# When VectorE's transposition and a pair of statistics take their turn: an edit of the spectrum phase in a convolution and recurrence kernel

## The chip, the cores and the metric

The kernel runs on one core of one Trainium2 chip. A core has five engines that work at the same time, each through its own queue of instructions in order: TensorE (PE in the profile, with PEld for its weight loads), VectorE (DVE), ScalarE (ACT), GpSimd (POOL) and SyncE (SP). Transfers between memory and the core's SBUF are issued from the queues of SP, ACT and POOL; an engine that must wait for another waits on a semaphore, and everything behind the waiting instruction in its queue waits too. The metric is the device time of one execution in microseconds (us); lower is better.

## The reference

The input x is 4 images of 64 channels and 256 by 256 pixels, all in float32. Two layers are added to it in turn. The edit lies in the first. Cut to what matters:

```python
def layer0(x):                                     # x + layer0(groupnorm(x))
    hidden = einsum('bchw,oc->bohw', x, w1)        # 1x1 convolution, 64 -> 384 channels
    hidden = depthwise_3x3(hidden, w_dw)
    q, k, v = split(hidden, 3, axis=1)             # 128 channels each
    out = irfft2(rfft2(patches_8x8(q)) * rfft2(patches_8x8(k)))   # circular convolution of each patch
    out = layernorm_over_channels(out) * ln_w + ln_b
    return einsum('bchw,oc->bohw', v * out, w_out) # 128 -> 64 channels
```

The second layer normalizes the result again in groups of channels and runs a recurrent cell (GRU) over the columns of the image; each column's state feeds the next. The group norm of an image needs the mean and variance of the whole image before the image's first pixel can be normalized.

## The kernel before, in words

The first layer takes about 3,600 us of the span and the second the rest. The first layer's loop is over 32 blocks (`for n in range(NBLK + 1)`, L617), 8 to an image; a block is 32 rows of the image, cut into 128 patches of 8 by 8 pixels with a halo of one pixel. The 3x3 convolution and the Fourier transform of a patch are one matrix product: for each channel a 100 by 64 matrix takes the patch with its halo to the 64 numbers of its spectrum. These matrices are streamed from memory (`fetch`, tile t).

A block goes through these phases, all in one program order:

1. First 1x1 phase (L632): 16 units, each a group of TensorE products into PSUM and one copy to the tile h, by ScalarE or, in two units, VectorE.
2. First spectrum phase (L657, `circular(n, 0, beside_first)`): four quarters, sp = 0 to 3. In each, TensorE transforms 16 channels of q and of k; ScalarE copies q's spectrum to a slot of the tile wk; VectorE makes two products of q and k (`products`, L400). After sp = 1 and after sp = 3 GpSimd adds the cross terms of two quarters (`crossed`, L410). After sp = 2 TensorE transforms the first two quarters back (`inverse`, L431).
3. Second 1x1 phase (L663): 16 units for the next channels. Unit 7 and unit 12 are copied by VectorE. After unit 11 the previous block's output is projected with w_out (`project`, L551) and VectorE adds the residual (`add_residual`, L568, four instructions); after unit 13 the rows leave for memory (`leave`, L579). Behind unit 15 comes the second inverse (`flush`).
4. Second spectrum phase (L679), third 1x1 phase (L683), and the phase of the values (L704).

PSUM is one ring of 8 banks (`psum`, L220). A transform or a unit takes two banks, an inverse or a projection four. TensorE can write a place again when whoever reads it is done. Followed through a block: the transform of k in quarter 3 takes the banks of k in quarter 2 and so waits for VectorE's two products of quarter 2. Units 14 and 15 of the second 1x1 phase take the four banks of the projection and wait for `add_residual`. The second inverse takes the banks of units 12 and 13 and waits for their copies.

Beside this main work VectorE does the layer norm of the *previous* block in small steps, one for each call of `go()` (L612). The generator `layer_norm` (L472) yields after each step; the last eight steps are transpositions, in turn of z and of v, for channel groups 0 to 3 (`turned`, L515). Seen from the first spectrum phase, z and v of groups 0 and 1 are done, and the four that are left are z2, v2, z3, v3. When group i is turned, `gated(n - 1, i)` (L527) scales z on ScalarE and multiplies it into v on GpSimd; the projection needs all four.

The third strand is the statistics of the *next* image, in blocks 0 to 23. GpSimd's queue fetches a piece of that image, 128 partitions by 1024 numbers, into one slot of wk called `seen` (`look`, L596). VectorE takes statistics of it with two instructions, and in the same call the next piece is fetched into the same slot:

```python
        def count(n, w):
            for i in range(2):
                nc.vector.bn_stats(bn0[:, w // 2 + i, :], seen[:, 512 * i : 512 * i + 512])
            if w == 12:
                nc.vector.bn_aggr(st0[:, n % 8, :], bn0)
            else:
                look(n, w + 4)
```

There are four pieces in a block: `look(n, 0)` stands at the block's start, and `count` at w = 0, 4, 8 and 12 in the first spectrum phase (sp = 1), the second 1x1 phase (unit 9), the second spectrum phase (sp = 2) and the third 1x1 phase (unit 2).

A class around the engines (`InOrder`, L146) keeps each engine's instructions in the order in which the program states them. Its method at L158 records every instruction, so the profile shows L158 for all of them; they are told apart by engine, operation and tiles (psring is the ring in PSUM; `bn<-wk` a statistic of `seen` or of rows that leave; `v<-v,z` the gate's product; `wk<-wk` a cross sum; `wk<-in_x` on POOL a `look`).

Of the kernel before, what the change touches and what calls it, by code (L numbers as in the profile page):

```python
# [163 lines left out]
def tile_conv_then_gru(  # L164
# [48 lines left out]
    with layer0 as s:  # L213
# [36 lines left out]
        def keep_matrices(queue, i, k0, k1):  # L250
            queue.dma_start(
                t_all[i, :, k0:k1].rearrange("p n k -> p (n k)"),
                ts[i][:, 16 * k0 : 16 * k1].rearrange("p c k -> p (c k)"),
            )
# [115 lines left out]
        def pointwise(n, chunk, unit, vector):  # L370

            unit_of(n, chunk, unit, vector)()
# [37 lines left out]
        def crossed(pair):  # L410

            slot = PAIRS[pair % 2][1]
            both = wk[:, slot : slot + 2]
            nc.gpsimd.tensor_tensor(both[:, :, 0:512], both[:, :, 0:512], both[:, :, 512:1024], ALU.add)
# [12 lines left out]
        def flush():  # L427
            while pending:
                pending.pop(0)()
# [97 lines left out]
        def gated(n, i):  # L527
            f = slice(32 * i, 32 * i + 32)
            nc.scalar.activation(
                z[:, :, f],  # L530
                z[:, :, f],
                AF.Identity,
                bias=ln_sb[:, 1, i : i + 1],
                scale=ln_sb[:, 0, i : i + 1],
            )
            nc.gpsimd.tensor_tensor(v[:, :, f], v[:, :, f], z[:, :, f], ALU.mult)
# [3 lines left out]
        def residual(n, u):  # L540
            b, r0 = n // 8, (n % 8) * 32 + u * 8
            xr = [wk[:, i].rearrange("p (r c) -> p r c", c=P) for i in (6, 2)]
            for g in range(2):
                for s in range(2):
                    nc.sync.dma_start(
                        xr[g][s * C : (s + 1) * C],
                        x[b, :, r0 + 16 * g : r0 + 16 * g + 8, s * P : s * P + P],
                    )
            return xr

        def project(n, u):  # L551
            po = psum(4)
            y = v.rearrange("p n (b k) -> p b n k", k=32)
            for b in range(4):
                for r in range(4):
                    for s in range(2):
                        n0 = 32 * u + 16 * s
                        nc.tensor.matmul(
                            po[s * 64 : s * 64 + 64, r].rearrange("p (n k) -> p n k", k=32),
                            lhsT=wo_sb[32 * r : 32 * r + 32, b, :],  # L560
                            rhs=y[32 * r : 32 * r + 32, b, n0 : n0 + 16],
                            start=b == 0,
                            stop=b == 3,
                            tile_position=(32 * r, s * 64),
                        )
            return po

        def add_residual(u, po, xr):  # L568
            for g in range(2):
                grid = xr[g].rearrange("p (h r) (n c) -> p h n r c", h=2, c=8)  # L570
                for half in range(2):
                    nc.vector.tensor_tensor(
                        grid[:, half],
                        po[:, 2 * g + half].rearrange("p (n r c) -> p n r c", r=4, c=8),
                        grid[:, half],
                        ALU.add,
                    )
# [18 lines left out]
        def look(n, w):  # L596

            nc.gpsimd.dma_start(seen, piece(x, n // 8 + 1, n % 8, w, 4))
# [8 lines that stand above are left out]
# [5 lines left out]
        def go(steps=1):  # L612
            for _ in range(steps):
                if norm:
                    next(norm, None)

        for n in range(NBLK + 1):  # L617
            last = n == NBLK
            more = not last and n // 8 + 1 < B
            if last:  # L620
                for _ in norm:
                    pass
                for i in range(4):
                    gated(n - 1, i)
                for u in range(2):
                    xr = residual(n - 1, u)
                    add_residual(u, project(n - 1, u), xr)
                    leave(n - 1, u, xr)
                break
            if more:  # L630
                look(n, 0)
            for unit in range(16):  # L632
                if unit < 14:
                    pointwise(n, 0, unit, unit in (3, 9) if norm else unit % 2)
                elif unit == 14:
                    last_two = [unit_of(n, 0, unit, False)]
                else:
                    last_two.append(unit_of(n, 0, unit, False))
                    for span in ((0, 16), (16, P)):
                        for copy in last_two:  # L640
                            copy(*span)
                if unit in (0, 3, 6, 9, 12):
                    go()
                if n == 0 and unit == 15:
                    keep_matrices(nc.gpsimd, 2, 0, 8)

            def beside_first(sp):
                if n and sp < 3:
                    gated(n - 1, sp)
                go()  # L650
                if n and sp == 3:
                    gated(n - 1, sp)
                if more and sp == 1:
                    count(n, 0)

            go()
            circular(n, 0, beside_first)  # L657
            crossed(1)
            go(8)
            xr = [None, None]  # L660
            if n:
                xr[0] = residual(n - 1, 0)
            for unit in range(16):  # L663
                pointwise(n, 1, unit, unit in (7, 12))
                if n and unit == 11:
                    add_residual(0, project(n - 1, 0), xr[0])
                if n and unit == 13:
                    leave(n - 1, 0, xr[0])
                if more and unit == 9:
                    count(n, 4)  # L670
            flush()
            norm = layer_norm(n)

            def beside(sp):
                go()
                if more and sp == 2:
                    count(n, 8)

            circular(n, 1, beside)  # L679
            image = None  # L680
            if n:
                xr[1] = residual(n - 1, 1)
            for unit in range(16):  # L683
                pointwise(n, 2, unit, unit in (4, 6, 15))
                if more and unit == 2:
                    count(n, 12)
                    if n % 8 == 7:
                        t = wk[:, 3]
                        nc.gpsimd.dma_start(t[:, 0 : 2 * P].rearrange("p (a q) -> p a q", a=2), sums)
                        image = norm_of_pieces(nc, st0, t, lambda: psum()[:, :, 0], eps, sc0[:, n // 8 + 1])  # L690
                if image and unit in (4, 8, 12):
                    next(image)
                if unit == 3:
                    flush()
                if unit in (6, 7):
                    go()
                if unit % 4 == 3 and n + 1 < NBLK:
                    load(n + 1, unit // 4)
            po = project(n - 1, 1) if n else None
            go(1)  # L700
            if n:
                add_residual(1, po, xr[1])
            go(3)
            for k in range(8):  # L704
                if k in (0, 3, 6):
                    pv = psum(4)
                    values(n, k, pv[:, 0:2])
                elif k in (1, 4, 7):
                    values(n, k, pv[:, 2:4])
                    keep_values(k - 1, 2, pv)  # L710
                else:
                    pv = psum()
                    values(n, k, pv)
                    keep_values(k, 1, pv)
                if k in (1, 2, 4) and n + 1 < NBLK:
                    normalize(n + 1, k // 2)
                if k == 5 and n:
                    leave(n - 1, 1, xr[1])
                if k == 5 and n + 1 < NBLK:
                    normalize(n + 1, 3)  # L720
                if k in (6, 7):
                    go()
            fetch(n * 24 + 28)
# [251 lines left out]
```

## Time and profile before

| | |
|---|---|
| median of 3 runs | 5094.03 us (5087.31 to 5103.36) |
| the profiled execution: its time, its span | 5097.92 us, 5096.1 us |
| granted TensorE clock, mean | 0.993 |
| PE matmuls busy | 4858.1 us, 95% |
| PEld weight loads busy | 4237.7 us, 83% |
| DVE busy | 4035.9 us, 79% |
| ACT busy | 3317.3 us, 65% |
| POOL busy | 1727.2 us, 34% |

The span is from the first to the last instruction of the profiled execution. Busy times of engines overlap. In a line of the timeline stand the start in us, the duration in us, the engine, the operation with the tile written, the arrow and the tiles read, shapes, the number of like instructions merged into the line, and in brackets how long the engine was idle just before and which engine's work ended that idle time.

### The profile page before, as it was taken

The numbers are of one execution on the slowest core, as the hardware profiler recorded it, in microseconds if no ns is written. First come the engines' busy times: TensorE is split into PE (matmuls) and PEld (weight loads), VectorE is DVE, ScalarE is ACT, GpSimd is POOL, SyncE is SP. The second block draws the span as 40 slices with busy tenths as digits, with TensorE's granted clock in tenths as the row PEclk, the third lists the DMA queues.
The fourth block names the chain that finished last, engine by engine and source line by source line (L and its number), as shares of the span: only waits on it lengthen the run. The fifth ranks groups of instructions, "written<-read, shape, count | busy, mean of one in ns | idle before, by whom it ended". The sixth has DMA issues, their size and how long they took to land.

```text
span 5096.1 us, 276113 instructions
## 1 busy us (share of the span) xinstructions
PE 4858.1 (95%) x127092; PEld 4237.7 (83%) x127092; DVE 4035.9 (79%) x7001; ACT 3317.3 (65%) x4269; POOL 1727.2 (34%) x1717
## 2 busy tenths in 40 slices
PE   6999999999999999999999999999879999999999
PEld 4888888888888888888888888888669999999998
DVE  5788888877888888788888877778867777777777
ACT  4666666666666666666666666666556666666665
POOL 0233333333333334333333333323343333333333
PEclk9999999999999999999999999999989999999999
DMA  8577676676777667677676666666443333333332
GB/s 306 162 189 191 186 191 182 180 183 187 187 195 196 170 184 187 179 190 191 186 195 168 173 161 174 173 171 180 121 125 103 104 103 103 102 104 103 103 103 73
DMA packets 435056, 823.57 MB, mean 162 GB/s; under 512 B 37156, under 2 KB 300068, under 8 KB 431364
## 3 DMA queue, kind: packets, MB, share of 16 engines
q1 hardware_dynamic: 380600, 582.13, 43.3%
q0 software_dynamic: 52432, 223.12, 14.7%
q8 instruction: 997, 16.33, 1.4%
q14 instruction: 163, 1.34, 0.1%
q10 hardware_dynamic: 864, 0.66, 0.0%
HBM read 660.53 MB, written 145.23 MB: 158 GB/s over the span
## 4 chain that ended last, share of the span: by engine, by line
PE 87%; ACT 4%; issue 4%; DVE 3%; DMA 2%; POOL 1%; SPq 0%; POOLq 0%; ACTq 0%; DVEq 0%
PE psring L158 62%; PE pshr L158 9%; PE pshz L158 8%; PE psni L158 6%; PE pshn L158 2%; ACT v L158 1%; ACT z L158 1%; DVE wk L158 1%; ACT xq L158 1%; DMA t<-t_all 1%; DVE z L158 1%; DMA t_all<-wk 0%; DVE lnst L158 0%; ACT h L158 0%; POOL v L158 0%
## 5 line engine op out<-in xcount | busy, mean ns | idle before, releaser
L158 PEld LDWEIGHTS psring<-h,t 100*32 100x32 f32 x49152 | 1385.9, 119 | 251.6 <-issue 214.5
L158 PE MATMUL psring<-h,t 100*32 100x128 f32 x49152 | 1463.5, 257 | 104.2 <-issue 69.4
L158 PEld LDWEIGHTS psring<-w_sb,xq 64*100 64x100 f32 x24576 | 1358.6, 163 | 107.9 <-issue 76.5
L158 PE MATMUL psring<-w_sb,xq 64*100 64x128 f32 x24576 | 1412.4, 271 | 23.0 <-issue 8.7
L158 ACT COPY h<-psring 100x1024 f32<-100x1024 f32 (+2 forms) x1371 | 1231.5, 990 | 308.0 <-PE psring L158 307.4
L158 DVE TENSOR_TENSOR wk<-psring,wk 128x1024 f32<-128x1024 f32 (+1 forms) x768 | 759.5, 1037 | 480.1 <-PE psring L158 346.4
L158 POOL TENSOR_TENSOR v<-v,z 128x2048 f32<-128x2048 f32 x128 | 582.9, 4558 | 664.5 <-DVE wk L158 603.5
L158 DVE TENSOR_TENSOR z<-z,moments 128x2048 f32<-128x2048 f32 x256 | 578.0, 2278 | 2.3
L158 POOL TENSOR_TENSOR wk<-wk 128x1024 f32<-128x1024 f32 x128 | 303.5, 2371 | 622.3 <-DVE wk L158 607.9
L158 POOL TENSOR_TENSOR raw<-raw,st 128x512 f32<-128x512 f32 x256 | 303.2, 1184 | 540.1 <-DVE st L158 424.6
L158 ACT COPY z<-psring 128x2048 f32<-128x2048 f32 (+1 forms) x144 | 248.4, 1725 | 343.9 <-PE psring L158 262.6
L158 ACT ACTIVATE z<-pshz,b_rz 128x288 f32<-128x288 f32 (+7 forms) x510 | 242.1, 475 | 339.2 <-PE pshz L158 334.1
L158 ACT COPY wk<-psring 128x1024 f32<-128x1024 f32 (+1 forms) x272 | 268.9, 988 | 288.5 <-PE psring L158 237.1
L158 PE MATMUL pshr<-st,wi 64*64 64x144 f32 (+7 forms) x12240 | 448.8, 270 | 6.9 <-DVE st L158 6.5
L158 PE MATMUL pshz<-st,wi 64*64 64x144 f32 (+7 forms) x12240 | 444.2, 269 | 0.9 <-issue 0.9
L158 PE MATMUL psni<-st,wi 64*64 64x144 f32 (+7 forms) x12240 | 444.0, 269 | 0.1
L158 DVE COPY h<-psring 100x1024 f32<-100x1024 f32 (+1 forms) x230 | 278.1, 1210 | 191.9 <-PE psring L158 188.1
L158 PEld LDWEIGHTS pshr<-st,wi 64*64 64x64 f32 x12240 | 378.0, 133 | 49.7 <-DVE st L158 36.9
L158 ACT COPY v<-psring 128x2048 f32<-128x2048 f32 (+2 forms) x176 | 251.9, 1436 | 254.3 <-PE psring L158 254.3
L158 DVE BATCH_NORM_STATS2 lnst<-z 128x6 f32<-128x128 f32 x2048 | 416.8, 281 | 0.0
L158 PEld LDWEIGHTS psni<-st,wi 64*64 64x64 f32 x12240 | 389.4, 133 | 21.9 <-issue 0.2
L158 PE MATMUL psring<-wk,g_sb 32*64 32x512 f32 x6144 | 386.7, 599 | 15.1 <-issue 12.1
(91 smaller groups left out, 6258.4 us busy)
## 6 DMA issues: line engine op xcount, KB each, us to landing
t<-t_all SPq DMA_DIRECT2D x768, 448.0 KB, 4.6
xq<-in_xh POOLq DMA_DIRECT2D x124, 800.0 KB, 5.2
wk<-in_x SPq DMA_DIRECT2D x256, 256.0 KB, 8.1
x<-wk POOLq DMA_DIRECT2D x256, 256.0 KB, 5.0
wk<-in_x POOLq DMA_DIRECT2D x96, 512.0 KB, 6.9
raw<-x SPq DMA_DIRECT2D x128, 256.0 KB, 3.0
raw<-x SPq DMA_DIRECT2D x256, 128.0 KB, 3.1
out<-raw SPq DMA_DIRECT2D x128, 256.0 KB, 2.7
```

The costliest lines, as they stand in the source:

```text
L158: return self.tc.keep_in_program_order(got(*args, **kwargs))
```

## The change

Two edits. In the first spectrum phase the four calls of `go()` become 0, 2, 1 and 1 steps: quarter 0 has none, and quarter 1 has two, so that the transposition of z2 stands behind the products of quarter 1, directly ahead of that of v2. And `count(n, 0)`, with its two statistics and the fetch of the next piece that it issues, moves from behind quarter 1 to behind unit 1 of the second 1x1 phase; `count(n, 4)` stays at unit 9. The first edit holds for blocks 1 to 31, the second for blocks 0 to 23. The computation is the same.

```diff
             def beside_first(sp):
                 if n and sp < 3:
                     gated(n - 1, sp)
-                go()
+                go((0, 2, 1, 1)[sp])
                 if n and sp == 3:
                     gated(n - 1, sp)
-                if more and sp == 1:
-                    count(n, 0)
...
                 if n and unit == 13:
                     leave(n - 1, 0, xr[0])
-                if more and unit == 9:
-                    count(n, 4)
+                if more and unit in (1, 9):
+                    count(n, unit // 9 * 4)
```

## The prediction

> **What bounds the kernel now.** I read the page's chain of work that ended last first, then the timeline of one block, engine by engine. Block 9, from 1107 us on, serves as the example.
>
> ```profile
> PE 87%; ACT 4%; issue 4%; DVE 3%; DMA 2%; POOL 1%; SPq 0%; POOLq 0%; ACTq 0%; DVEq 0%
> ```
>
> TensorE holds 87% of the chain. An edit on VectorE or GpSimd moves the time only where TensorE waits for it, so I look for those places in TensorE's own timeline:
>
> ```profile
> 1107.71 10.86 PE L158 MATMUL psring<-h,t 100*32 100x128 f32 x384 [0.36 <-ACT h L158]
> 1118.51 1.97 PE L158 MATMUL psring<-wk,g_sb 32*64 32x512 f32 x32
> 1120.94 1.16 PE L158 MATMUL psring<-wk,g_sb 32*64 32x512 f32 x16 [0.46 <-POOL wk L158]
> 1122.03 3.98 PE L158 MATMUL psring<-h,t 100*32 100x128 f32 x128
> 1125.94 10.83 PE L158 MATMUL psring<-w_sb,xq 64*100 64x128 f32 x192
> 1136.71 3.69 PE L158 MATMUL psring<-v,wo_sb 32*64 32x512 f32 x64
> 1140.33 3.79 PE L158 MATMUL psring<-w_sb,xq 64*100 64x128 f32 x64
> 1144.13 2.83 PE L158 MATMUL psring<-wk,g_sb 32*64 32x512 f32 x48
> ```
>
> These are the first spectrum phase (six transforms, the inverse in two parts, two transforms), units 0 to 11 of the second 1x1 phase, the projection, units 12 to 15 and the second inverse. The only waits in 40 us are 0.46 us for GpSimd's cross sum, and the last two transforms, 3.98 us where other blocks show 3.70. VectorE over the same stretch:
>
> ```profile
> 1111.55 2.36 DVE L158 TENSOR_TENSOR wk<-psring,wk 128x1024 f32<-128x1024 f32 x2 [1.28 <-PE psring L158]
> 1113.83 2.30 DVE L158 STREAM_TRANSPOSE z<-z 128x2048 f32<-128x2048 f32 x1
> 1116.05 2.32 DVE L158 TENSOR_TENSOR wk<-psring,wk 128x1024 f32<-128x1024 f32 x2
> 1118.29 2.29 DVE L158 STREAM_TRANSPOSE v<-v 128x2048 f32<-128x2048 f32 x1
> 1120.51 1.24 DVE L158 BATCH_NORM_STATS2 bn<-wk 128x6 f32<-128x512 f32 x2
> 1121.67 2.34 DVE L158 TENSOR_TENSOR wk<-psring,wk 128x1024 f32<-128x1024 f32 x2
> ...
> 1134.43 1.28 DVE L158 BATCH_NORM_STATS2 bn<-wk 128x6 f32<-128x512 f32 x2
> 1140.46 2.48 DVE L158 TENSOR_TENSOR wk<-psring,wk 128x512 f32<-128x512 f32 x4 [4.75 <-issue]
> ```
>
> The last two lines are today's second count (unit 9) and the four residual adds, which start 0.07 us after the projection's end at 1140.39. GpSimd, behind its cross sum for quarters 0 and 1:
>
> ```profile
> 1125.35 0.60 POOL L158 DMA_DIRECT2D wk<-in_x  x1
> 1125.97 4.55 POOL L158 TENSOR_TENSOR v<-v,z 128x2048 f32<-128x2048 f32 x1
> 1130.89 4.51 POOL L158 TENSOR_TENSOR v<-v,z 128x2048 f32<-128x2048 f32 x1 [0.37 <-DVE v L158]
> 1135.35 2.38 POOL L158 TENSOR_TENSOR wk<-wk 128x1024 f32<-128x1024 f32 x1
> 1137.65 0.58 POOL L158 DMA_DIRECT2D wk<-in_x  x1
> ```
>
> The first fetch brings the piece that unit 9 counts; two gate products, the second of which waits for the transposition of v3, and a cross sum stand between it and the next fetch.
>
> **Part 1: the transposition and the first count leave their places in the spectrum phase.** After the change the products of quarter 1 wait only for k's second transform. TensorE needs 3.49 us for a q and k pair, so in block 9 that ends at 1114.9, and products start 0.14 us behind a transform (as the first did): 1115.05 instead of 1116.05. They take 2.36 us, to 1117.4, one us earlier than now. Then z2 and v2 follow in steps of 2.23 us, and the products of quarter 2 start at 1117.4 - 0.1 + 4.46 = 1121.8, against 1121.67 now: what the statistics give back (1.16 us, 1120.51 to 1121.67), the idle us between quarters 0 and 1 takes. The earlier cross sum removes TensorE's 0.46 us, but the last transform of k waits for the products of quarter 2 anyway, which end 0.1 us later: +0.1 us in this block. I did this sum for every block from its own transform ends, and took away the cross sum's wait wherever it had ended that pause: -0.6 to +1.0 us, in all +2 us for blocks 1 to 23. In blocks 24 to 31 there is no count to take away and the products of quarter 2 come about 1.4 us later; most have over a us of room there (in block 25, k's last transform starts 1.14 us after it could), and they sum to +1 us. Ends: -7 us if nothing waited for the products of quarter 2, +31 if each block lost a whole us. I take +3. Behind the waiting instructions, ScalarE's scaling of z2 slides 2 us (to 1119.8) into a gap that ends at 1122.23, and v3 keeps its time behind quarter 3.
>
> **Part 2: the fetch that the moved count issues.** VectorE's two statistics move to behind v3, where it idles 2.57 us before the copy of unit 7: 1.24 us, hidden (with that cover gone, at most 1.24 us a block). But their fetch moves too, on GpSimd's queue past both gate products and the second cross sum. The freed 0.60 us there helps nothing, since the last gate product waits for v3. So the piece for unit 9 is now issued where the *following* piece is issued today, at 1137.65 instead of 1125.35. VectorE meets the count of that piece after its copy of unit 7, at 1134.43, and must stop until it lands. The fetch at this place:
>
> ```profile
> wk<-in_x POOLq DMA_DIRECT2D x1, 512.0 KB, 4.0
> ```
>
> It lands at 1141.61. Two statistics, 1.20 us to the next start, and 0.02 for the wake-up (as in block 4, landing at 610.80, start at 610.82) put the residual adds at 1142.83 instead of 1140.46: 2.37 us late. Queued behind are the adds and the copy of unit 12. TensorE finishes units 12 and 13 at 1142.2, waits about 1.9 us for two adds before unit 14, 0.3 us for the other two before unit 15, and then for the copy of unit 12 before the second inverse, which starts at 1146.5 instead of 1144.13. Now nothing lies between VectorE and TensorE there: the inverse starts 0.05 us after that copy ends. The same sum over blocks 1 to 23, each with its own fetch and projection, gives 1.63 us (block 8) to 3.51 us (block 14), mean 2.43: 23 x 2.43 = 56 us. Block 0 has no gates and no projection and loses nothing; blocks 24 to 31 have no counts. The third fetch is now issued after the second count, some 6 us later, but its count is 20 us away.
>
> How long the landing takes is the term to weigh. The Trainium skill ("DMA: Bandwidth & Descriptors", Anatomy of one DMA) puts a transfer from GpSimd's queue at 2.0 us and its bytes over 436 GB/s: an estimate of 3.2 us for 512 KB, and 56 - 23 x 0.75 = 39 us. The page's median over all these fetches is 6.9 us, which would make 56 + 23 x 2.9 = 123 us. I take the rows of the same place, 3.8 to 5.4 us, since the same work lies around it.
>
> **Part 3: TensorE's clock.** A new pause can also cost clock. The Trainium skill ("TensorE: Matmul & The Clock Gate", What's actually happening) lets the clock fall to half after an idle window of about 3.4 us; the pauses here, 1.2 to 3.0 us in front of unit 14, would not do it, and the sum would be 5094 + 59 = 5153. The trace is stricter. This is block 21 right behind a pause of 1.82 us:
>
> ```profile
> 2472.78:2477.27 4.49, 4.49 (x41) 1.75 (x44) 4.29 (x3) 0.00 (x0) 4.47 (x3) 0.62 0.17 48
> ```
>
> The clock is 0.62 over 4.49 us, so 4.49 x 0.38 = 1.7 us are lost. Of five pauses between 1.74 and 1.93 us in the first layer this one alone did it. The new ones are as long and have 0.3 us more close behind; I take one in three of 23: 8 x 1.7 = 14 us. Ends: 0 and 39.
>
> **The sum.** 56 + 14 + 3 = 73 us on the profiled execution's span of 5096.1, whose own time was 5097.92; the median of the runs is 5094.03, 0.1% below, and I add to that: **5167 us**, 1.4% slower.
>
> **Rivals.**
> - *Given back later.* The view of waits puts 108.8 us of TensorE's pauses down to issue, about 1 us of it 6 to 11 us into each spectrum phase. If the queued instructions pile up during the new pause, these could shrink. Against it: in the slower 1x1 phases they could pile up already, and the pause comes back all the same. If all of one us returned in 23 blocks, and the clock held: 5094 + 56 + 3 - 23 = 5130.
> - *The pause costs more.* The clock halves in all 23 blocks (5192), or the fetch lands as slowly as its median elsewhere (5234). For it: SP's fetches of matrices and residual rows share the transfer engines. Against: in this block they were quiet from 1137 on.
> - *Not slower: the count is hidden and only the earlier cross sum remains.* It needs the piece on chip by 1139.2, that is issued 2.4 us sooner; then the pause is gone, and the earlier cross sum's full worth is -7 us: 5087. From there on any earlier issue decides it. What speaks for it is GpSimd's 0.60 us and the cross sum one us sooner; what speaks against it is that the last gate product starts 0.17 us after v3's end, and v3 stands behind the products of quarter 3, which don't come earlier.
>
> **How the numbers follow.** A measurement of this kernel tells 0.3%, 15 us, from no change. Forecast 0.68; given back 0.10; costs more 0.14; not slower 0.08, of which 0.06 within 0.3% and 0.02 faster by a gain in the spectrum phase that I don't see. All the rest is slower, 0.92. The range reaches from the given-back case, 5130, to a little over the case of 23 halved windows, 5198, and leaves out the 6.9 us landing and the hidden count.
>
> **What would show it.** In the changed profile: VectorE idle before `bn<-wk` on the transfer `wk<-in_x`, about 7 us a block where now 41.3 us in all are; two fetches one after the other on GpSimd behind the cross sum, the second after VectorE's statistics; the residual adds 2.4 us after the projection's end instead of 0.07; a pause of TensorE before unit 14; the inverse's wait for the cross sum gone in the first spectrum phase, with the products of quarter 2 where they were; more half-clock windows. The prediction is wrong if the adds still start at the projection's end, or if the spectrum phase gets shorter by more than half a us.

## The result, and the profile after

The changed kernel takes 5165.93 us, the median of 4 runs (5159.99 to 5172.56), against 5093.72 us for the kernel before (4 runs, the three above and one more): a ratio of 1.0135, with a 95% interval of 1.0118 to 1.0151. The forecast was 5167. The profiled execution's span is 5164.8 us, 68.7 more than before.

The page's chain of work that ended last, by engine, in the changed kernel:

```profile
PE 77%; DVE 8%; issue 6%; ACT 4%; DMA 3%; POOL 1%; DVEq 0%; SPq 0%; POOLq 0%; ACTq 0%
```

TensorE fell from 87% to 77% of it; VectorE rose from 3% to 8%, DMA and issue by 3 points together. The page's group of statistics (instructions, then busy time and mean duration, then idle time just before them and what ended it) says where VectorE's part begins:

```profile
L158 DVE BATCH_NORM_STATS2 bn<-wk 128x6 f32<-128x512 f32 x448 | 279.6, 677 | 200.5 <-DMA wk<-in_x 200.5
```

VectorE stands still for the piece of the next image for 200.5 us. The view of waits has this wait in both kernels, before and after (us in total, times, longest):

```profile
DVE bn L158 <- DMA wk<-in_x: 41.3, 18, 3.8
DVE bn L158 <- DMA wk<-in_x: 200.5, 41, 7.7
```

Block 9 is the prediction's example; here are the same stretches in the changed kernel. VectorE's timeline:

```profile
1135.30 2.35 DVE L158 TENSOR_TENSOR wk<-psring,wk 128x1024 f32<-128x1024 f32 x2 [0.83 <-PE psring L158]
1138.78 2.35 DVE L158 TENSOR_TENSOR wk<-psring,wk 128x1024 f32<-128x1024 f32 x2 [1.13 <-ACT wk L158]
1141.05 2.30 DVE L158 STREAM_TRANSPOSE z<-z 128x2048 f32<-128x2048 f32 x1
1143.27 2.27 DVE L158 STREAM_TRANSPOSE v<-v 128x2048 f32<-128x2048 f32 x1
1145.47 2.31 DVE L158 TENSOR_TENSOR wk<-psring,wk 128x1024 f32<-128x1024 f32 x2
...
1154.74 1.25 DVE L158 BATCH_NORM_STATS2 bn<-wk 128x6 f32<-128x512 f32 x2
1157.39 1.23 DVE L158 COPY h<-psring 100x1024 f32<-100x1024 f32 x1 [1.41 <-PE psring L158]
1166.30 1.29 DVE L158 BATCH_NORM_STATS2 bn<-wk 128x6 f32<-128x512 f32 x2 [7.68 <-DMA wk<-in_x]
1167.51 2.46 DVE L158 TENSOR_TENSOR wk<-psring,wk 128x512 f32<-128x512 f32 x4
```

The first five lines are the spectrum phase: VectorE idles 1.13 us between the products of quarters 0 and 1 (the line names ScalarE, but its copy ended at 1137.98; k's second transform ended at 1138.65, so this is the wait that was forecast), and the products of quarter 2 start 10.17 us after those of quarter 0, where they started 10.12 after. The first count has moved behind v3, into an idle stretch. Then, behind the copy of unit 7, 7.68 us of waiting for the transfer, and only then the residual adds. GpSimd's queue in the same block, and the landing of the first fetch in it (window 1161.6 to 1162.2, us from issue to landing last):

```profile
1154.98 4.51 POOL L158 TENSOR_TENSOR v<-v,z 128x2048 f32<-128x2048 f32 x1 [2.34 <-ACT h L158]
1159.44 2.37 POOL L158 TENSOR_TENSOR wk<-wk 128x1024 f32<-128x1024 f32 x1
1161.74 0.61 POOL L158 DMA_DIRECT2D wk<-in_x  x1
1167.90 0.53 POOL L158 DMA_DIRECT2D wk<-in_x  x1 [5.55 <-DVE bn L158]
```

```profile
wk<-in_x POOLq DMA_DIRECT2D x1, 512.0 KB, 4.5
```

The fetch stands where the third one stood, 2.3 us behind the start of the second cross sum, although its statistics had been done since 1156. TensorE, from the spectrum phase on:

```profile
1142.52 3.95 PE L158 MATMUL psring<-wk,g_sb 32*64 32x512 f32 x48
1146.40 3.72 PE L158 MATMUL psring<-h,t 100*32 100x128 f32 x128
1150.04 10.73 PE L158 MATMUL psring<-w_sb,xq 64*100 64x128 f32 x192
1160.70 3.69 PE L158 MATMUL psring<-v,wo_sb 32*64 32x512 f32 x64
1164.32 1.99 PE L158 MATMUL psring<-w_sb,xq 64*100 64x128 f32 x32
1168.23 3.81 PE L158 MATMUL psring<-w_sb,xq 64*100 64x128 f32 x32 [1.92 <-DVE wk L158]
1171.98 3.33 PE L158 MATMUL psring<-wk,g_sb 32*64 32x512 f32 x48
```

The inverse's wait for the cross sum is gone. In its place, two units after the projection, stands a pause of 1.92 us that VectorE ends. The two units behind it take 3.81 us instead of 1.99. That isn't the clock alone; in block 3, which has no half-clock window, they take 2.90:

```profile
472.41 2.90 PE L158 MATMUL psring<-w_sb,xq 64*100 64x128 f32 x32 [1.16 <-DVE wk L158]
```

In block 9 unit 14 starts 0.72 us after the four adds do (in block 3, 0.73), behind the first of them and not behind two; in all 23 blocks it starts 0.05 or 0.06 us after the first add's end. That the two units then take 0.9 us more fits a wait for the other adds inside them. For the clock, a row of the view by stretches (length, busy time of PE, PEld, DVE, ACT and POOL, then the granted clock, DMA share and GB/s) covers block 9:

```profile
1164.39:1172.00 7.61, 5.55 (x68) 4.60 (x68) 5.70 (x9) 2.02 (x2) 3.35 (x5) 0.85 0.44 129
```

The clock is 0.85 over 7.61 us. The records of the clock show one window of 3.41 us at half speed, from 1169.67 to 1173.08, so it reaches into the second inverse.

From the start of each phase on TensorE to that of the next, blocks 0 to 30, the changed profile against that of before:

| stretch of a block | change, sum in us |
|---|---|
| first spectrum phase | +0.8 (blocks 1 to 23: -1.9) |
| units 0 to 11 and the projection | -3.8 |
| units 12 to 15, to the start of the second inverse | +63.1 |
| second inverse | +3.7 |
| second spectrum phase | +5.6 |
| third 1x1 phase, values, first 1x1 phase | +2.2 |

The stretches add up to 71.6 us; the span grew by 68.7, as the rest of the program was 2.9 us shorter. Of this, 66.8 us lie in the one place that the prediction named.

### The profile page after: what moved, and what is told of

Its sections match the earlier page's. It is cut to its first block, busy times and chain, and to the rows that moved or that the text cites. A ratio compares the mean times of both kernels' runs of the same rounds, so it can differ in the third digit from the quotient of the medians.

```text
span 5164.8 us, 276114 instructions
## 1 busy us (share of the span) xinstructions
PE 4894.7 (95%) x127092; PEld 4247.9 (82%) x127092; DVE 4037.1 (78%) x7001; ACT 3327.2 (64%) x4269; POOL 1726.4 (33%) x1717
## 4 chain that ended last, share of the span: by engine, by line
PE 77%; DVE 8%; issue 6%; ACT 4%; DMA 3%; POOL 1%; DVEq 0%; SPq 0%; POOLq 0%; ACTq 0%
PE psring L158 52%; PE pshr L158 8%; PE pshz L158 8%; PE psni L158 6%; DVE wk L158 3%; PE pshn L158 2%; DMA wk<-in_x 2%; DVE v L158 2%; ACT v L158 1%; DVE z L158 1%; ACT z L158 1%; ACT xq L158 1%; POOL wk L158 1%; DMA t<-t_all 1%; DMA t_all<-z 1%
## 5 line engine op out<-in xcount | busy, mean ns | idle before, releaser
L158 PE MATMUL psring<-w_sb,xq 64*100 64x128 f32 x24576 | 1439.5, 272 | 56.0 <-DVE wk L158 37.2
L158 DVE BATCH_NORM_STATS2 bn<-wk 128x6 f32<-128x512 f32 x448 | 279.6, 677 | 200.5 <-DMA wk<-in_x 200.5
```

The lines of the kernel that those rows point to most:

```text
L158: return self.tc.keep_in_program_order(got(*args, **kwargs))
```

## The experiments

The runs beside these were on a chip where the kernel before took 5104.76 to 5106.97 us; so ratios are compared, and times as differences from that kernel.

**The first edit alone.** z2 moves behind the products of quarter 1; the count stays in quarter 1.

```diff
-                go()
+                go((0, 2, 1, 1)[sp])
```

> The first edit alone: z2 stands behind the products of quarter 1, and the count with its fetch stays there too, behind z2 and v2. My theory has the loss in the fetch, which keeps its place on GpSimd's queue ahead of the second and third gate product here, so the residual adds should start at the projection's end again (0.07 us). But nothing makes up for VectorE's idle us between quarters 0 and 1 now: the products of quarter 2 end 1.16 us later than in the changed kernel, and the sum over the blocks' own transform ends gives +20 us for blocks 1 to 23 and +1 for the others: 5094 + 21 = 5115. Rival, the transposition is what costs: the whole 72 us stay, 5166. Rival, it is harmless: 5094.

Measured: ratio 1.0050 (1.0033 to 1.0068), 25 us over the kernel before. The adds start 0.05 us after the projection, so nothing of the large loss comes from here. The loss that there is sits where it was put: the first spectrum phase is 21.8 us longer in all. TensorE and VectorE in its block 9:

```profile
1131.25 1.95 PE L158 MATMUL psring<-h,t 100*32 100x128 f32 x64
1134.14 1.96 PE L158 MATMUL psring<-h,t 100*32 100x128 f32 x64 [0.94 <-DVE wk L158]
```

```profile
1130.58 1.25 DVE L158 BATCH_NORM_STATS2 bn<-wk 128x6 f32<-128x512 f32 x2
1131.74 2.34 DVE L158 TENSOR_TENSOR wk<-psring,wk 128x1024 f32<-128x1024 f32 x2
```

The last transform of k waits 0.94 us for the products of quarter 2, which stand behind two transpositions and the statistics and end at 1134.08.

**The second edit alone.** z2 back behind quarter 0; the first count with its fetch behind unit 1.

```diff
-                go((0, 2, 1, 1)[sp])
+                go()
```

> The second edit alone: z2 back behind quarter 0, the first count with its fetch behind unit 1 of the second 1x1 phase. My theory: the fetch lands as late as in the changed kernel, so the residual adds start about 2.5 us after the projection in blocks 1 to 23 (59 us), some ten half-clock windows follow (17 us), and the spectrum phase gains 2 to 3 us from VectorE's freed 1.16 us: 5094 + 59 + 17 - 3 = 5167, within 10 us of the changed kernel. Rival, the two edits together make the loss (the transposition delays v3 and so the last gate product): then this one alone is well under 5140.

Measured: ratio 1.0117 (1.0093 to 1.0142), 68 us by the medians; the interval overlaps the changed kernel's. In block 9 VectorE waits as it does in the changed kernel:

```profile
1172.59 1.29 DVE L158 BATCH_NORM_STATS2 bn<-wk 128x6 f32<-128x512 f32 x2 [7.69 <-DMA wk<-in_x]
1173.80 2.47 DVE L158 TENSOR_TENSOR wk<-psring,wk 128x512 f32<-128x512 f32 x4
```

The adds start 2.63 us after the projection in the mean (2.62 in the changed kernel), 59 us in 23 blocks, and units 12 to 15 are 67.1 us longer. So the moved count makes the loss by itself. The spectrum phase is 7.5 us shorter, more than the 2 to 3 expected; 2.9 of it are block 21, whose half-clock window in the kernel before did not come.

**The same fetch on another queue.** The changed kernel, with the fetch of the moved count issued from SyncE.

```diff
-        def look(n, w):
+        def look(n, w, queue=nc.gpsimd):
...
-            nc.gpsimd.dma_start(seen, piece(x, n // 8 + 1, n % 8, w, 4))
+            queue.dma_start(seen, piece(x, n // 8 + 1, n % 8, w, 4))
...
-                look(n, w + 4)
+                look(n, w + 4, nc.gpsimd if w else nc.sync)
```

> The changed kernel, with the fetch that the moved count issues put on SyncE's queue instead of GpSimd's. VectorE's and TensorE's order is the same. If the place on GpSimd's queue, behind the gate products and the cross sum, is what makes the piece late, it is now issued at the end of the statistics, some 5.5 us sooner, behind the residual rows on SyncE's queue; those land about 1.5 us before the projection's end, so the piece should be 0 to 1.5 us late: 5094 + 3 + 0 to 35, I say 5110. Rival, the transfer itself is the limit, in whatever queue it stands (the transfer engines are busy with residual rows and matrices): 5150 or more.

Measured: ratio 0.9999 (0.9988 to 1.0010). The whole loss is gone, a little more than I had expected. VectorE in its block 9:

```profile
1134.25 1.25 DVE L158 BATCH_NORM_STATS2 bn<-wk 128x6 f32<-128x512 f32 x2
1136.89 1.23 DVE L158 COPY h<-psring 100x1024 f32<-100x1024 f32 x1 [1.40 <-PE psring L158]
1140.53 1.29 DVE L158 BATCH_NORM_STATS2 bn<-wk 128x6 f32<-128x512 f32 x2 [2.41 <-DMA wk<-in_x]
1143.95 2.48 DVE L158 TENSOR_TENSOR wk<-psring,wk 128x512 f32<-128x512 f32 x4 [2.13 <-issue]
```

VectorE still waits for the piece, 2.41 us, but the statistics behind it are done 2.13 us before the adds can start. Order of VectorE and TensorE, size and count of transfers are the changed kernel's; only the queue differs. Nor is the transfer faster on this queue: from its issue to the statistics pass 3.7 to 5.3 us over 23 blocks (5.0 in block 9), where it landed 3.8 to 4.7 us after its issue from GpSimd's. In block 9 it is issued 5.7 us sooner, counted from the start of the second 1x1 phase. So the transfer is not the limit, its place behind GpSimd's work is.

**The second count later.** The changed kernel, with the second count behind unit 14 instead of unit 9.

```diff
-                if more and unit in (1, 9):
-                    count(n, unit // 9 * 4)
+                if more and unit in (1, 14):
+                    count(n, unit // 14 * 4)
```

> The changed kernel, with the second count moved from behind unit 9 to behind unit 14 of the second 1x1 phase. The fetch is as late as in the changed kernel, at its place on GpSimd's queue, but VectorE meets it only after the residual adds, the copy of unit 12 and the statistics of the rows that leave, where it is idle for 4.28 us. If the loss is VectorE standing still ahead of the adds, all of it goes, the half-clock windows with it: 5094 + 3 = 5097. Rival, the late fetch hurts in some other way (GpSimd's stores, transfers that collide with the matrices of the second spectrum phase): 5120 or more.

Measured: ratio 1.0033 (1.0022 to 1.0044), 19 us, where I expected 3. The adds are on time (0.06 us after the projection in every block) and units 12 to 15 lost nothing; in block 9 VectorE now takes the second count behind them, six statistics in one line:

```profile
1137.68 2.48 DVE L158 TENSOR_TENSOR wk<-psring,wk 128x512 f32<-128x512 f32 x4 [5.95 <-PE psring L158]
1141.21 3.65 DVE L158 BATCH_NORM_STATS2 bn<-wk 128x6 f32<-128x512 f32 x6
```

So the wait ahead of the adds was the large loss, but the rival has a part: the second spectrum phase is 25.0 us longer. TensorE's timeline there, in blocks 8 and 9:

```profile
1042.05 3.70 PE L158 MATMUL psring<-h,t 100*32 100x128 f32 x128 [1.44 <-DMA t<-t_all]
1148.24 3.70 PE L158 MATMUL psring<-h,t 100*32 100x128 f32 x128 [0.43 <-issue]
1154.44 4.01 PE L158 MATMUL psring<-h,t 100*32 100x128 f32 x128 [2.50 <-issue]
```

TensorE's pauses in that phase of blocks 1 to 23 add up to 39.7 us here, against 21.5 in the kernel before, where nearly all are put down to issue, and 22.0 in the changed kernel. Of the 39.7, about 28 are put down to issue and 11.1, in 13 blocks, to the transfer of a matrix (t), as in block 8; the kernel before has no such wait in this phase. The clock adds to it: five of these phases have a half-clock window here, none in the kernel before. The second count now issues the third fetch at 1145.15, one us into this phase.

**The same without the third fetch.**

```diff
-            else:
+            elif w != 4:
                 look(n, w + 4)
```

> The kernel with the second count behind unit 14, but without the fetch that this count issues: the third piece isn't loaded, and the third count takes the statistics of the second piece again (this part of the computation is left out). If what was left of the loss there, 19 us, comes from this fetch running into the matrix loads and the instruction fetches at the start of the second spectrum phase, it goes: ratio 0.999 to 1.001, and TensorE's pauses in that phase shrink to what they were. Rival, it is VectorE's two late statistics or something else: the ratio stays at 1.003.

Measured: ratio 0.9986 (0.9974 to 0.9998). The 19 us are gone, and the pauses in the second spectrum phase are 25.4 us. In its block 9 they read:

```profile
1158.41 3.69 PE L158 MATMUL psring<-h,t 100*32 100x128 f32 x127 [0.40 <-issue]
1163.24 0.27 PE L158 MATMUL psring<-h,t 100*32 100x128 f32 x1 [1.14 <-issue]
```

It is this fetch, run into the start of that phase, and not VectorE's late statistics. One way in which it does so is in the trace, the matrices that come late: 11.1 us of such waits with the fetch, 0.3 without. How the rest comes about is argued only. In block 9 of the late-count kernel a 16 KB transfer of the instruction queue starts at 1151.92, just as TensorE stops at 1151.94 between two transforms, and takes 1.18 us among others; TensorE goes on at 1154.44. That its instructions came late fits, but no run separated this.

**A longer wait.** The changed kernel, with one more instruction on GpSimd ahead of the moved fetch.

```diff
             else:
+                if w == 0:
+                    nc.gpsimd.tensor_tensor(seen, seen, seen, ALU.add)
                 look(n, w + 4)
```

> The changed kernel, with one more instruction on GpSimd between the moved statistics and the fetch that follows them: it adds the slot of the piece to itself, in place, and the fetch then overwrites it. The same form over 1024 columns takes 2.37 us on GpSimd. Nothing else moves. My theory: VectorE stands still for the piece, TensorE for VectorE, one for one: 23 x 2.37 = 55 us more than the changed kernel, so 73 + 55 = 128 us over the kernel before with the clock as it is. And if it is TensorE's pause in front of unit 14 that halves the clock, pauses of about 3.7 us instead of 1.3 do it in nearly every one of the 23 blocks instead of about ten: up to 20 us more, about 145 over the kernel before (ratio 1.028). Rival, half-clock windows have nothing to do with this pause: their number stays near 11, ratio 1.025. Rival, part of the pause is given back later: under 1.022.

Measured: ratio 1.0266 (1.0245 to 1.0287), 140 us by the medians. The adds start 4.77 us after the projection in the mean, 2.15 more than in the changed kernel for an instruction of 2.37 (in block 9 its two GpSimd adds, the cross sum and this one, take 4.20 together). No part is given back. The time lies between both forecasts for the clock; the records of the clock decide. TensorE's timeline and the view by stretches, block 9:

```profile
1186.98 1.99 PE L158 MATMUL psring<-w_sb,xq 64*100 64x128 f32 x32
1193.57 3.83 PE L158 MATMUL psring<-w_sb,xq 64*100 64x128 f32 x32 [4.59 <-DVE wk L158]
```

```profile
1191.00:1200.00 9.00, 6.43 (x80) 4.37 (x80) 7.18 (x11) 2.02 (x2) 3.35 (x5) 0.81 0.58 156
```

With pauses of 3.31 us and more before unit 14, each of the 23 blocks has a half-clock window there (0.81 over 9.00 us is one of 3.41). In the changed kernel, with 1.10 to 2.14 us, 6 of 23 have one; in the kernel before, and in each one whose adds are on time, none. What the windows cost: units 12 to 15 and the second inverse are 143.7 us longer here, the adds 108.4 us later, and 35 us over 23 windows are 1.5 us each, an estimate that puts all the rest down to the clock.

The traces also tell which of the short pauses bring a window. Within each of the nine profiles all half-clock windows of the first layer begin on one grid of 3.413 us, to within a nanosecond, whatever the pauses. These rows follow that grid in the changed kernel, two steps of block 2 (pause 1.23 us) and three of block 14 (pause 2.14 us):

```profile
353.88:357.29 3.41, 1.97 (x24) 1.35 (x22) 3.41 (x7) 1.25 (x2) 1.67 (x3) 1.00 0.29 53
357.29:360.71 3.42, 3.42 (x38) 1.99 (x44) 3.26 (x5) 1.79 (x2) 1.68 (x3) 0.50 0.95 274
1739.69:1743.11 3.42, 2.38 (x45) 1.78 (x32) 0.83 (x2) 0.99 (x1) 0.00 (x0) 1.00 0.33 128
1743.11:1746.52 3.41, 2.10 (x26) 1.67 (x28) 3.41 (x6) 0.58 (x2) 1.26 (x2) 1.00 0.38 96
1746.52:1749.93 3.41, 3.39 (x62) 1.38 (x59) 2.94 (x5) 1.47 (x2) 2.10 (x3) 1.00 0.90 249
```

The short pause lies within one step, which leaves TensorE idle for 1.44 us of it, and the next step is at half clock. The long one falls across two steps, with 1.04 and 1.31 us idle, and the steps behind these stay at full clock. Over the first layers of all nine profiles (from 130 us on, to the last block's second spectrum phase), each of the 47 steps with 1.83 us idle or more was followed by a half-clock window, none of the 9093 with less than 1.2 was, and 30 of the 183 between were.

**The count alone, its fetch on SyncE.** The second edit and the queue of the third experiment together.

```diff
-                go((0, 2, 1, 1)[sp])
+                go()
...
-                look(n, w + 4)
+                look(n, w + 4, nc.gpsimd if w else nc.sync)
```

The new parameter of `look` is as in the third experiment.

> The second edit alone (z2 stays behind quarter 0), with the moved count's fetch on SyncE's queue. Where the count alone lost 67 us in front of the residual adds, nothing is left of that if the place on GpSimd's queue made it, as on SyncE's queue the adds started at the projection's end. VectorE's freed 1.16 us in the spectrum phase stays; with the count alone it was worth 6 us in blocks 1 to 23. So I expect 4 to 8 us under the kernel before, ratio 0.9985 to 0.999. Rival, the transfer on SyncE's queue delays the matrices: ratio 1.000 or more.

Measured: ratio 0.9980 (0.9970 to 0.9990), 10 us under the kernel before by the medians. It is the fastest complete version here, faster than both kernels. The gain is small, 0.1 to 0.3%; the interval lies below 1, but the 10 us are within the 15 that the prediction takes as the limit of what can be told. In blocks 1 to 23 of its profile the first spectrum phase is 4.5 us shorter and units 0 to 11 with the projection 5.5; in all, the span of this one execution was not shorter than that of before (it was the slowest of its 14 runs), so the profile doesn't say where all of it comes from.

## Why the prediction was right, point by point

- **Part 1, the spectrum phase: right.** +3 us forecast, +0.8 measured over blocks 0 to 30. The idle us between quarters 0 and 1 came, 1.13 us in block 9, and the freed statistics paid for it: the products of quarter 2 moved by 0.05 us, forecast 0.1. The transposition alone, without that payment, lengthens this phase by 21.8 us, where the same sum gave 21. The sum of +0.8 is two single blocks and luck: block 0, which has no transpositions and waits for its first matrices, became 3.6 us longer, and block 21 2.8 us shorter, as its half-clock window in the kernel before (1.7 us) did not come again. The other 29 blocks together changed by about nothing, where the forecast had +3.
- **Part 2, the fetch: right, in place and size.** Adds late by 2.43 us in the mean was the forecast, 56 us; measured 2.56, and 59 us. Block 9 itself lost 3.05, not 2.37, as its landing took 4.5 us instead of 4.0 and its issue stood 0.1 us later behind the projection's start. The landing was the term with the widest ends. The rows of the same place, 3.8 to 5.4 us, were the right ones: the moved fetch lands in 3.8 to 4.7 us, median 3.9. The estimate of 3.2 us from the Trainium skill ("DMA: Bandwidth & Descriptors", Anatomy of one DMA) was too short, the page's median of 6.9 too long; that median is made by fetches which meet other traffic, and on the whole page it fell to 4.6 after the change because one fetch in four left that traffic.
- **Part 3, the clock: right that short pauses do it, the size too large.** 8 windows and 14 us forecast; 6 windows, and about 8 us (63.1 + 3.7 less the adds' 58.8), measured from unit 12 to the end of the second inverse. One step of the sum was wrong: unit 14 waits for one add, not two, so the pauses before it were 1.10 to 2.14 us where 1.2 to 3.0 were forecast; the rest of the loss lies inside units 14 and 15. The changed profile has 11 windows in the first layer where that of before has one, but the other five stand elsewhere, in later phases behind pauses put down to issue; the other kernels whose adds were on time have 2 to 7 of them. They differ from profile to profile, and no run shows that this change made them. The idle 3.4 us that the prediction cites from the Trainium skill ("TensorE: Matmul & The Clock Gate", What's actually happening) are not needed: pauses of 1.23 and 1.29 us had a window behind them, while one of 2.14 us had none, and from 3.31 us on all had. The forecast of one in three came from five pauses of the kernel before; it depends on where a pause falls on the grid shown above.
- **Not in the sum:** units 0 to 11 became 3.8 us shorter, and in every other profile in which the first count and its fetch moved they are 3.3 to 5.5 us shorter, but not with the transposition alone (+0.9). That the fetch no longer runs beside them fits; no run separates it from the count's move. The other stretches, +5.6 and +2.2 us, hold the five windows named above, at up to 1.7 us each. These errors nearly cancelled: with the adds' 59, the clock's 8 and the rest, the forecast's 73 met 72 by the medians (68.7 by the two spans) by some luck in its smaller terms.
- **The rivals.** Given back later: no, TensorE's pauses in the second spectrum phase stayed, 22.0 against 21.5 us, and a pause 2 us longer came through in full. Not slower, the count hidden: false for this change, but the pause is gone from the point that was named; the 7 us of gain that were to follow did not show (ratio 0.9999). Issued on SyncE, the piece is there 2.1 us before it is needed, and the loss is gone.

## What to carry to other kernels

A transfer's time begins where its issue stands in a queue that works in order; moving a consumer moves the issue of its *next* transfer past everything in that queue, and its slack must be worked out from there. Here that was two gate products and a cross sum, and it cost 1.35%. Before a small task is moved off a busy phase, look at what it issues and from which engine; a queue without long work, as SyncE's here, would have made the same edit harmless. And a pause of the bounding engine can cost more than its length where it brings the clock down, here by about 1.5 us for each half-clock window.

## What was not expected of the hardware

TensorE's clock halved for one window of 3.41 us behind pauses as short as 1.23 us, in 6 of 23 blocks, and behind pauses of 3.31 us and more in 23 of 23. What decided it was not the length of the pause alone but how much of it fell into one step of a grid of 3.413 us: with 1.83 us or more, always. And a single 512 KB fetch, moved to the start of a phase in which matrices stream in, cost TensorE 14 to 18 us of pauses in 23 blocks (39.7 us against 25.4 without it and 21.5 before), although nothing waited for its data; 11.1 us of them were waits for the matrices.
